# Selective-scan layer of a four-layer kernel: where the gate is multiplied, who splits B, which activation tables are loaded, how many variance buffers there are

## The chip, the cores and the metric

The kernel runs on one core of a Trainium2 chip. The metric is the device time of one launch in microseconds (us). One launch computes four layers one after the other; the change is in the first.

## What is computed

Four layers map x, of shape 8 x 64 x 64 x 64 (images, channels, rows, columns), to the output. Layer 0 is a selective scan over the 4096 places of each image, followed by a gated norm; layers 1 and 3 are attention layers, layer 2 adapts a small network by gradient steps. What matters here is layer 0's core (cut):

```python
xz = jnp.einsum('bhwc,dc->bhwd', x, in_proj_w) + in_proj_b      # x is layer-normed
xi, z = jnp.split(xz, 2, axis=-1)                               # 128 channels each
xc = jax.nn.silu(_dwconv3(jnp.transpose(xi, (0, 3, 1, 2)), conv_w, conv_b))
...                       # xs: four directions (rows, columns, and both reversed)
x_dbl = jnp.einsum('bkdl,kcd->bkcl', xs, xproj_w)
dts, Bs, Cs = jnp.split(x_dbl, [R, R + N], axis=2)              # R = 4, N = 16
dts = jax.nn.softplus(jnp.einsum('bkrl,kdr->bkdl', dts, dtproj_w) + dtproj_b)
# for each place t, channel c and state n:
h = h * jnp.exp(dt_t[..., None] * A) + dt_t[..., None] * B_t[:, :, None, :] * u_t[..., None]
y = jnp.einsum('bkcn,bkn->bkc', h, C_t)
...
y = _ln(y, outnorm_g, outnorm_b, LN_EPS) * jax.nn.silu(z)       # the gate
return jnp.einsum('bhwd,cd->bhwc', y, outproj_w) + outproj_b
```

## The kernel before, in words

**Units and steps.** `scan_layer` works on eight images. Each has four directions k (in the order 0, 2, 1, 3; the last image 1, 3, 0, 2), and each direction four chunks of 1024 places: 16 steps per image. A step handles the 16 states n one by one; each is a unit on tiles of 128 channels x 1024 places:

- `load` (L729): one row of B (`bt`) or C (`ct`) is read from DRAM and spread over 128 partitions, 512 KB; SyncE's queue issues it, five buffers for `ct`, two for `bt`.
- `decay` (L733): ScalarE computes a = exp(dt * A_n), three buffers.
- `spread` (L751): TensorE makes B_n on all partitions out of three bf16 parts of B (`bs`, 48 rows) into the PSUM tile z, two buffers. For the states in `BY_POOL` (0, 3, 6, 8) GpSimd multiplies `bt` by dt*u instead (`product`, L741) and ScalarE copies that to z (L748).
- `unit` (L778, L782, L787): VectorE multiplies z by dt*u (not for `BY_POOL`), then scans h = a*h + z; GpSimd multiplies h by `ct`.
- `sum_up` (L848): TensorE adds the result to the PSUM tile `yps`, two units later; `save_state` (L769) keeps the last column for the next chunk.

The order of work is written out by hand (`tc.manual_schedule()`): every engine gets its instructions in the order of the program. The main loop runs ahead for some operations (`spread` one unit, `decay` two, `product` three).

**Background.** Everything else hangs in a queue of small items (`Background`). In each unit at most one item gives TensorE its matmuls (`make`, called in `bg.before`), and one unit later its result is used (`use`, in `bg.after`); what was put off with `bg.later` goes out in the `bg.after` of the same unit for a `make`, one unit later for a `use`. In the units listed in `idle` (6, 7, 8) no item with a `make` is taken. Items share two PSUM banks (tag `mm`). They are, in the order of an image: eight loads of x into `xn` and its layer norm (`norm_x`), the projection into the padded image `pad`, the gates, the convolutions in groups of nine taps (L544) with Silu (L553), and, when the next image has begun (step 0, unit 4), the norm and output of the finished one (`after`, `norm_y`).

**The gate before.** `gate(j)` (L520 on): a matmul of win and the block of `xn` (L524), Silu on ScalarE (L529) into an SBUF tile z, which goes by DMA to the DRAM tile `zd`. Eight blocks per image, before the convolutions. In `after`, `load` brings a block of `zd` back (and a block of x, `xr`), GpSimd multiplies it by the normed y (L580), and `project_out` (L586, L587) adds x by the identity and multiplies by wout.

**The norm of y.** `inverse_root`: for each block a row of variances is put from PSUM into the SBUF tile `vrow` (L344, ScalarE) and sent to DRAM (L345, one unit later). That tile shares the tag `rstd`, with one buffer, with the row that is read back. Then the variances are read as 128 partitions, Sqrt (L355), reciprocal (L358), and back. `norm_y` multiplies y by the inverse root (L460, VectorE, out of PSUM) and applies gain and offset (L461).

**The next step's inputs.** `prepare` queues `project` as the first items of a step: B and C (`dps`, L619, for k < 2, which also serves k + 2), dt as Relu and Abs (L647, L648). In the units 6, 7, 8 the rest of softplus follows: exp (L653), ln(1 + .) (L656), the sum on GpSimd (L659); dt*u at unit 11 (L678). For k < 2 `pieces` splits B into three bf16 parts in the units 7 to 13: fetch (L687), first part (L691, ScalarE), remainder (L695, GpSimd), second part (L698, ScalarE), third (L701, GpSimd), store (L706), get (L713). In the first three steps of image 0 (`early`) all of this stands in the units 12 to 15.

**Tables.** [...] These loads are placed by the compiler: in the code before one at each ln, one at the exp after it, one at each Silu and Sqrt and one at the exp after these.

Of the kernel before, what the change touches and what calls it, by code (L numbers as in the profile page):

```python
# [10 lines left out]
F32 = mybir.dt.float32  # L11
# [7 lines left out]
NB = 8  # L19
# [222 lines left out]
def scan_layer(cm, x_in, w, xh):  # L242

    tc, nc = cm.tc, cm.nc
    with ExitStack() as ctx:
# [73 lines left out]
        eps = cm.tile([128, 1], "eps")  # L319
        nc.vector.memset(eps, 1e-5)  # L320
        pick = cm.pool.tile([3 * N, N], BF16, name="pick", tag="pick")
        rows = work.tile([3 * N, N], F32, name="rows", tag="vsm")
# [5 lines left out]
        nc.gpsimd.memset(pad, 0.0)  # L328
        bg = Background()

        def bank(name):
# [4 lines left out]
        def inverse_root(nb):  # L336

            var = dr.tile([L], F32, name="vard", tag="vard")[: nb * BK]
            rs = dr.tile([L], F32, name="rsd", tag="rsd")[: nb * BK]
            sm = {}  # L340

            def put(ps, n, at):
                t = work.tile([NBK, BK], F32, name="vrow", tag="rstd", bufs=1)
                nc.scalar.copy(t[:n], ps[:n])  # L344
                bg.later(lambda: nc.sync.dma_start(  # L345
                    var[at * BK : (at + n) * BK].rearrange("(o n) -> o n", o=n), t[:n]
                ))

            def fetch(_):

                sm["v"] = work.tile([128, TQ], F32, name="vsm", tag="vsm")[:, : nb * BK // 128]
                nc.sync.dma_start(sm["v"], var.rearrange("(p f) -> p f", p=128))

            def root(_):
                nc.scalar.activation(sm["v"], sm["v"], AF.Sqrt, bias=eps)  # L355

            def invert(_):
                nc.vector.reciprocal(sm["v"], sm["v"])  # L358
                bg.later(lambda: nc.sync.dma_start(rs.rearrange("(p f) -> p f", p=128), sm["v"]))

            def back(_):
                sm["r"] = work.tile([NBK, BK], F32, name="rstd", tag="rstd", bufs=1)[:nb]
                nc.sync.dma_start(sm["r"], rs.rearrange("(j f) -> j f", j=nb))

            chain = [none, (None, fetch), none, none, (None, root), (None, invert), none]
            chain += [(None, back), none, none, none]
            return put, chain, sm
# [57 lines left out]

        def norm_y(y, blocks, load, multiply, project_out):

# [7 lines left out]
            def variance(j):  # L435
                def make():
                    ps = bank("vps1")
                    nc.tensor.matmul(
                        ps[:1], lno_avg[:, NBK - 1 : NBK], sq.pop(j), start=True, stop=True
                    )  # L440
                    return ps

                def use(ps):
                    put(ps, 1, j - j0)
                    if j + 2 in blocks:
                        square(j + 2)

                return make, use

            def apply(j):  # L450
# [7 lines left out]
                def use(ps):  # L458
                    v = y[:, bass.ts(j, BK)]
                    nc.vector.tensor_tensor(v, v, ps, ALU.mult)  # L460
                    nc.scalar.activation(v, v, AF.Identity, bias=on_b, scale=on_g)  # L461
                    if j - 1 in blocks:
                        multiply(j - 1)

# [3 lines left out]
            for j in blocks:  # L468
                out.append(variance(j))
                if j in blocks[1:6:2] or nb == 2:  # L470
                    at = j if nb == 2 else j0 + (j - j0) // 2
                    out.append((None, lambda _, at=at: load(at)))
            out += chain
            out += [apply(j) for j in blocks[:2]]
            end = (None, lambda _: multiply(blocks[-1]))
            if nb == 2:
                out += [end, none]
            for j in blocks:
                if j + 2 in blocks:
                    out.append(apply(j + 2))  # L480
                    if j + 2 == blocks[-1]:
                        out.append(end)
                out += [project_out(j), none]
            return out
# [4 lines left out]
        def before(b):  # L489

            xn = io.tile([2 * C, NBK // 2, BK], F32, name="xn", tag="xn", bufs=1)

# [3 lines left out]
            u = io.tile([DI, L], F32, name="u", tag="u")  # L496
            zd = dr.tile([DI, L], F32, name="zd", tag="zd")
            rows = BK // S
# [6 lines left out]
            def project_in(j):  # L505
# [6 lines left out]
                def use(ps):  # L512
# [3 lines left out]
                    )  # L516

                return make, use

            def gate(j):  # L520
                def make():
                    ps = bank("zps")
                    half, x = block(j)
                    nc.tensor.matmul(ps, win[half, 1, :], x, start=True, stop=True)  # L524
                    return ps

                def use(ps):
                    z = work.tile([DI, BK], F32, name="z", tag="z", bufs=3)
                    nc.scalar.activation(z, ps, AF.Silu, bias=inb[:, 1:2])  # L529
                    bg.later(lambda: nc.sync.dma_start(zd[:, bass.ts(j, BK)], z))  # L530

                return make, use

            def convolve(j):
# [17 lines left out]
                def use(_):  # L552
                    nc.scalar.activation(u[:, bass.ts(j, BK)], held[0], AF.Silu, bias=convb)  # L553
                    if b:
                        bg.done[b] += 1
# [6 lines left out]
            for pairs in FIRST if b == 0 else (range(NBK // 2),):  # L562
                items.append(norm_x(b, xn, pairs, project_in))
            return u, zd, items, [gate(j) for j in range(NBK)], [convolve(j) for j in range(NBK)]

        def after(b, y, zd, blocks=range(NBK)):

# [3 lines left out]
            def load(j):  # L571
                xr = work.tile([C, BK], F32, name="xr", tag="xr", bufs=3)
                nc.sync.dma_start(xr, xf[:, bass.ts(j, BK)])
                z = work.tile([DI, BK], F32, name="z", tag="z", bufs=3)
                nc.sync.dma_start(z, zd[:, bass.ts(j, BK)])
                gated[j] = (xr, z)

            def multiply(j):
                z = gated[j][1]
                nc.gpsimd.tensor_tensor(z, z, y[:, bass.ts(j, BK)], ALU.mult)  # L580

            def project_out(j):
                def make():
                    po = bank("ops")
                    xr, z = gated[j]
                    nc.tensor.matmul(po[:C], cm.ident[:C, :C], xr, start=True, stop=False)  # L586
                    nc.tensor.matmul(po[:C], wout, z, start=False, stop=True)  # L587
                    return po
# [10 lines left out]

            return norm_y(y, blocks, load, multiply, project_out)  # L600

# [78 lines left out]

        def pieces(ctl, low):

# [31 lines left out]

            return ([fetch, first, subtract, second, third, store] if ctl["k"] < 2 else []) + [get]

# [152 lines left out]
        def prepare(b, s):  # L869
# [18 lines left out]
            )  # L888
            ctl["pieces"] = pieces(ctl, low)
            return ctl  # L890
# [5 lines left out]
        def start(b):  # L896
            u, zd, items, gates, convs = before(b)
            images[b] = {"u": u, "zd": zd}
            bg.add(items[0] + items[1])
            if b == 0:  # L900
                bg.add(convs[0] + convs[1])
                for s in range(1, NCH):
                    later[s] = sum(items[s + 1 : s + 2], []) + convs[2 * s] + convs[2 * s + 1]
                later[NCH] = gates
            else:
                bg.done[b] = 0
                bg.add([(None, lambda _: bg.groups.extend(deque(conv) for conv in convs))])
                bg.add(gates)


        with tc.manual_schedule():
            start(0)
            bg.drain()
# [13 lines left out]
            for b in range(NB):  # L927
                for s in range(4 * NCH):
# [29 lines left out]
                    for n in range(N):  # L958
# [30 lines left out]
                        if s == 0 and n == LAG + 2 and b > 0:  # L989
                            last = images.pop(b - 1)  # L990
                            bg.add(after(b - 1, last["row"], last["zd"]))
                            bg.add([(None, lambda _, b=b - 1: bg.flushed.add(b))])
                        if late and n == LAG + 2:
                            c = 4 * NCH - s
                            bg.add(after(b, images[b]["row"], images[b]["zd"], range(2 * c, 2 * c + 2)))
                        if s == (1 if b else NCH) and n == 0 and b + 1 < NB:
                            bg.add(later.pop(NCH, []))
                            start(b + 1)
# [8 lines left out]
            last = images[NB - 1]  # L1007
            bg.add(after(NB - 1, last["row"], last["zd"], range(2)))
            bg.drain()
# [1148 lines left out]
```

## Time and profile before

| | us |
|---|---|
| median of three runs | 12334.72 (12313.69 to 12336.37) |
| profiled execution | 12328.75, its span 12326.7 |
| scan layer in the span | 0 to 7053: before the first scan 94.4, eight images 920.8, 853.4, 856.3, 847.7, 859.6, 849.9, 871.6, 864.9, after the last scan 34.4 |
| other three layers | 5273.7 |
| busy in the span: PE, DVE, ACT, POOL | 11203.1, 10359.2, 7820.8, 7399.3 |
| middle of the scan layer (1500 to 6500 us): DMA | 64% busy, 207 to 215 GB/s |

In all views PE is TensorE (PEld its weight loads), DVE VectorE, ACT ScalarE, POOL GpSimd and SP the SyncE queue that issues all the DMAs. A group's row gives line, engine, operation, output and inputs with their shapes, the count, then busy time in us and mean in ns, then the idle time just before these instructions with what ended it. A window's row gives its bounds and length, the busy time of each engine with the number of instructions, the clock granted to TensorE, the DMA share and GB/s. A timeline row gives start, duration, engine, line and operation, with the idle time before it in brackets. Windows of images and steps begin at the first scan of each.

### The profile page before, as it was taken

The page shows a single profiled execution, that of the slowest core. Times are in us where ns is not written, and L with a number is a line of the kernel's source. Part 1 is how long each engine was busy: PE and PEld are TensorE (multiplying, and loading weights), DVE is VectorE, ACT ScalarE, POOL GpSimd, SP SyncE. Part 2 cuts the span into 40 slices and gives each one's busy share as a digit, 9 for nine tenths or more (in the row PEclk, how much of TensorE's full clock was granted, in tenths as well). Part 3 has the DMA queues.
Part 4 walks back from the last instruction along what each step waited for, and adds up shares of the span by engine and source line. Part 5 has one row for each costly group of instructions (what it writes and reads, how often), then busy time and mean ns, then how long its engine had stood idle before and what let it go on. Part 6 is the DMA issues. An engine that isn't in the chain of part 4 may idle for free. (4 is left out here: it accounts for less than half of the span.)

```text
span 12326.7 us, 120038 instructions
## 1 busy us (share of the span) xinstructions
PE 11203.1 (91%) x38827; PEld 4075.9 (33%) x38827; DVE 10359.2 (84%) x7334; ACT 7820.8 (63%) x10409; POOL 7399.3 (60%) x3510
## 2 busy tenths in 40 slices
PE   7899999999999999999998899999987779999999
PEld 2233332332332332333322233232335463333333
DVE  5999999999999999999999776868677686676767
ACT  4776776776766766767766554646547574555554
POOL 5999999999999999999999700000006480000000
PEclk8999999999999999999999899999998789999999
DMA  3666666666666666666666400000011100000000
GB/s 115 207 213 218 209 209 217 219 203 216 218 210 213 211 210 217 213 215 213 199 213 211 164 24 26 5 25 7 17 41 41 41 21 24 19 4 19 5 11 6
DMA packets 541331, 1562.16 MB, mean 127 GB/s; under 512 B 127360, under 2 KB 144400, under 8 KB 538128
## 3 DMA queue, kind: packets, MB, share of 16 engines
q1 hardware_dynamic: 540688, 1554.36, 38.5%
q8 instruction: 309, 5.06, 0.2%
q14 instruction: 334, 2.74, 0.1%
HBM read 1456.41 MB, written 88.87 MB: 125 GB/s over the span
## 5 line engine op out<-in xcount | busy, mean ns | idle before, releaser
L787 POOL TENSOR_TENSOR ct<-ct,h 128x1024 f32<-128x1024 f32 x2048 | 4794.6, 2364 | 248.2 <-DVE h L782 113.3
L782 DVE TENSOR_TENSOR_SCAN h<-a,state,z 128x1024 f32<-128x1024 f32 x1536 | 3573.1, 2342 | 118.2 <-ACT z L748 67.1
L1159 DVE TENSOR_TENSOR sum<-sum,ex 128x1024 f32<-128x1024 f32 x1920 | 2347.5, 1223 | 618.1 <-ACT ex L1152 484.4
L1152 ACT ACTIVATE ex<-sc 128x1024 f32<-128x1024 f32 x2048 | 1968.1, 1024 | 1359.6 <-PE sc L1147 1359.6
L848 PE MATMUL yps<-ct,ident 128*128 128x512 f32 x5632 | 2809.0, 630 | 2.5 <-POOL ct L787 2.4
L733 ACT ACTIVATE a<-dt,amat 128x1024 f32<-128x1024 f32 x2048 | 2345.4, 1147 | 725.9 <-DVE h L782 712.5
L778 DVE TENSOR_TENSOR z<-z,e 128x1024 f32<-128x1024 f32 x1536 | 1863.3, 1213 | 221.1 <-PE z L751 143.2
L1166 PE MATMUL av<-ex,v 128*64 128x512 f32 x8192 | 1950.0, 604 | 0.0
L1147 PE MATMUL sc<-q,k 16*128 16x512 f32 (+1 forms) x8192 | 1562.2, 623 | 4.2 <-ACT q L1140 3.1
L848 PEld LDWEIGHTS yps<-ct,ident 128*128 128x128 f32 x5632 | 1006.4, 194 | 1384.2 <-issue 1220.6
L751 PE MATMUL z<-bs,pick 48*128 48x512 bf16 x3072 | 948.0, 389 | 536.5 <-DVE h L782 485.5
L848 PE MATMUL yps<-ct,lno_cen 128*128 128x512 f32 x2560 | 1276.3, 630 | 0.0
L782 DVE TENSOR_TENSOR_SCAN h<-a,z 128x1024 f32<-128x1024 f32 x512 | 1162.7, 2282 | 81.4 <-ACT z L748 57.2
L741 POOL TENSOR_TENSOR bt<-bt,e 128x1024 f32<-128x1024 f32 x512 | 1210.1, 2364 | 5.3 <-DMA bt<-bc 5.3
L1473 POOL TENSOR_TENSOR gt<-gt,pad 128x1024 f32<-128x1024 f32 x16 | 34.9, 2179 | 1570.2 <-ACT gt L1472 1570.2
L1166 PEld LDWEIGHTS av<-ex,v 128*64 128x64 f32 x8192 | 512.2, 136 | 1332.8 <-issue 1278.9
L1147 PEld LDWEIGHTS sc<-q,k 16*128 16x128 f32 (+1 forms) x8192 | 528.4, 184 | 1016.2 <-issue 977.3
L748 ACT COPY z<-bt 128x1024 f32<-128x1024 f32 x512 | 519.8, 1015 | 537.5 <-POOL bt L741 334.8
L751 PEld LDWEIGHTS <-pick 48*128 48x128 bf16 x3072 | 177.6, 95 | 1754.9 <-DVE h L782 1003.0
L848 PEld LDWEIGHTS yps<-ct,lno_cen 128*128 128x128 f32 x2560 | 458.1, 193 | 618.3 <-issue 564.2
L544 PE MATMUL vps<-pad,convd 128*128 128x512 f32 x1152 | 550.9, 602 | 12.9 <-ACT e L648 12.9
L1846 DVE RECIPROCAL r<-e 128x512 f32<-128x512 f32 x128 | 420.7, 3323 | 0.0
(416 smaller groups left out, 10449.5 us busy)
## 6 DMA issues: line engine op xcount, KB each, us to landing
ct<-bc SPq DMA_DIRECT2D x2048, 512.0 KB
bt<-bc SPq DMA_DIRECT2D x512, 512.0 KB
x<-x SPq DMA_DIRECT2D x12, 2048.0 KB
bc<-e SPq DMA_DIRECT2D x128, 128.0 KB
zd<-z SPq DMA_DIRECT2D x64, 256.0 KB
z<-zd SPq DMA_DIRECT2D x64, 256.0 KB
x<-x SPq DMA_DIRECT2D x32, 512.0 KB
part<-x SPq DMA_DIRECT2D x128, 128.0 KB
```

The lines of the kernel that those rows point to most:

```text
L544: nc.tensor.matmul(held[0].rearrange("p (r c) -> p r c", c=S), convd[:, t, :], pad[:, j * rows + dy : (j + 1) * rows + dy, dx : dx + S], s ...
L733: ctl["exp", n] = nc.scalar.activation(ctl["a", n], ctl["dt"], AF.Exp, scale=amat[:, ctl["k"], n : n + 1])
L741: nc.gpsimd.tensor_tensor(bt, bt, ctl["dus"], ALU.mult)
L751: nc.tensor.matmul(z[:, bass.ts(i, BK)], pick[:, n : n + 1].to_broadcast([3 * N, DI]), ctl["bs"][:, bass.ts(i, BK)], start=True, stop=True,)
L778: first = nc.vector.tensor_tensor(z, z, ctl["dus"], ALU.mult)
L782: nc.vector.tensor_tensor_scan(h[:, flip], a[:, flip], z[:, flip], 0.0 if state is None else state[:, n : n + 1], ALU.mult, ALU.add,)
L787: freed[at] = nc.gpsimd.tensor_tensor(ct, ct, h, ALU.mult)
L848: nc.tensor.matmul(ctl["ps"][:, bass.ts(i, BK)], ctl["mat"], ct[:, bass.ts(i, BK)], start=False, stop=(n == N - 1 and not ctl["turns"]),)
L1147: nc.tensor.matmul(sc[:, e, :], k[r : r + d, bass.ts(j, 128)], qs[i][r : r + d, :], start=True, stop=True,)
L1152: nc.scalar.activation(ex, sc, AF.Exp)
L1159: nc.vector.tensor_tensor(sums[i], sums[i], ex, ALU.add)
L1166: nc.tensor.matmul(avs[i][r, :], v[:, j, r], ex[:, e, :], start=(j == 0), stop=(j == TQ - 1))
```

## The change

Five edits, all in `scan_layer`:

1. The gate is no longer computed ahead and kept in DRAM. `gate(j)` moves into `after`: the matmul goes to a PSUM bank, Silu is applied in place in PSUM (put off with `bg.later`, so after the decay of the same unit), and one unit later VectorE multiplies y by it out of PSUM. `zd` and both its DMAs are gone, and `xn` has two buffers, since it is needed until then.
2. For k < 2 (but not in the early steps) B's second and third parts are made by TensorE: identity times B minus the parts so far (`minus`, bf16), then copied by ScalarE to bf16. The pieces stand at the units 5, 7, 8, 9, 10 and 13, and unit 9 is idle for the background too.
3. `exp_and_ln` loads the set of tables with exp and ln; it is called at the start and after each Silu and Sqrt. In the changed program no other load stands before an exp or an ln.
4. `vrow` has a tag of its own with two buffers; `inverse_root`'s chain has one empty item fewer.
5. The order of the items in `norm_y` follows: loads of `xr` inside the first three variances, a gate between the norm of a block and its output.

```diff
+        minus = cm.pool.tile([128, 128], BF16, name="minus", tag="minus")
+        nc.vector.tensor_scalar(minus, cm.ident, -1.0, None, ALU.mult)
...
+        def exp_and_ln():
+
+            nc.scalar.add_instruction(mybir.InstLoadActFuncSet(
+                name=nc.get_next_instruction_name(), act_func_set_id=6, engine=mybir.EngineType.Activation,
+                ins=[], outs=[],
+            ))
...
             def put(ps, n, at):
-                t = work.tile([NBK, BK], F32, name="vrow", tag="rstd", bufs=1)
+                t = work.tile([NBK, BK], F32, name="vrow", tag="vrow", bufs=2)
...
                 nc.scalar.activation(sm["v"], sm["v"], AF.Sqrt, bias=eps)
+                exp_and_ln()
...
-            chain += [(None, back), none, none, none]
+            chain += [(None, back), none, none]
...
                     if j + 2 in blocks:
                         square(j + 2)
+                    if j - j0 < 3:
+                        load(j)
...
-                    if j - 1 in blocks:
-                        multiply(j - 1)
...
-            out += [apply(j) for j in blocks[:2]]
-            end = (None, lambda _: multiply(blocks[-1]))
-            if nb == 2:
-                out += [end, none]
+            out += [apply(j) for j in blocks[:2]] + [gate(j0)]
             for j in blocks:
                 if j + 2 in blocks:
                     out.append(apply(j + 2))
-                    if j + 2 == blocks[-1]:
-                        out.append(end)
-                out += [project_out(j), none]
+                out += [gate(j + 1) if j + 1 in blocks else none, project_out(j)]
...
-            xn = io.tile([2 * C, NBK // 2, BK], F32, name="xn", tag="xn", bufs=1)
+            xn = io.tile([2 * C, NBK // 2, BK], F32, name="xn", tag="xn")
...
-                def use(ps):
-                    z = work.tile([DI, BK], F32, name="z", tag="z", bufs=3)
-                    nc.scalar.activation(z, ps, AF.Silu, bias=inb[:, 1:2])
-                    bg.later(lambda: nc.sync.dma_start(zd[:, bass.ts(j, BK)], z))
...
                     nc.scalar.activation(u[:, bass.ts(j, BK)], held[0], AF.Silu, bias=convb)
+                    exp_and_ln()
...
-                z = work.tile([DI, BK], F32, name="z", tag="z", bufs=3)
-                nc.sync.dma_start(z, zd[:, bass.ts(j, BK)])
-                gated[j] = (xr, z)
-
-            def multiply(j):
-                z = gated[j][1]
-                nc.gpsimd.tensor_tensor(z, z, y[:, bass.ts(j, BK)], ALU.mult)
+                gated[j] = xr
+
+            def gate(j):
+                def make():
+                    ps = bank("zps")
+                    half, x = block(j)
+                    nc.tensor.matmul(ps, win[half, 1, :], x, start=True, stop=True)
+
+                    def silu():
+                        nc.scalar.activation(ps, ps, AF.Silu, bias=inb[:, 1:2])
+                        exp_and_ln()
+
+                    bg.later(silu)
+                    return ps
+
+                def use(ps):
+                    v = y[:, bass.ts(j, BK)]
+                    nc.vector.tensor_tensor(v, ps, v, ALU.mult)
...
+            def rest(i):
+                def do():
+                    ps = bank("brps")
+                    b, p = (low[n] for n in "bp")
+                    nc.tensor.matmul(ps[:, :256], cm.ident, b.rearrange("p a x -> p (a x)"), start=True, stop=False)
+                    for q in range(i):
+                        nc.tensor.matmul(
+                            ps[:, :256], minus, p[:, q].rearrange("p a x -> p (a x)"),
+                            start=False, stop=(q == i - 1),
+                        )
+                    nc.scalar.copy(p[:, i].rearrange("p a x -> p (a x)"), ps[:, :256])
+
+                return do
+
+            if ctl["k"] >= 2:
+                return [get]
+            if early:
+                return [fetch, first, subtract, second, third, store, get]
+            return [fetch, first, rest(1), rest(2), store, get]
...
-                    idle = () if early or late else (6, 7, 8)
+                    parts = nxt and not early and nxt["k"] < 2
+                    idle = () if early or late else (6, 7, 8, 9) if parts else (6, 7, 8)
...
-                            hooks = {14 - len(do) + i: [f] for i, f in enumerate(do)}
+                            hooks = dict(zip((5, 7, 8, 9, 10, 13) if parts else (13,), ([f] for f in do)))
```

More of the change, by code (lines that the diff above doesn't have):

```diff
@@ L424, in norm_x, with norm_y @@
             return out
-        def norm_y(y, blocks, load, multiply, project_out):
+        def norm_y(y, blocks, load, gate, project_out):
             put, chain, sm = inverse_root(len(blocks))
@@ L469, in norm_y @@
                 out.append(variance(j))
-                if j in blocks[1:6:2] or nb == 2:
-                    at = j if nb == 2 else j0 + (j - j0) // 2
-                    out.append((None, lambda _, at=at: load(at)))
             out += chain
-            out += [apply(j) for j in blocks[:2]]
-            end = (None, lambda _: multiply(blocks[-1]))
-            if nb == 2:
-                out += [end, none]
+            out += [apply(j) for j in blocks[:2]] + [gate(j0)]
             for j in blocks:
@@ L496, in before @@
             u = io.tile([DI, L], F32, name="u", tag="u")
-            zd = dr.tile([DI, L], F32, name="zd", tag="zd")
             rows = BK // S
@@ L516, in use @@
                     )
[L518 to L525, printed above, removed]
-                def use(ps):
-                    z = work.tile([DI, BK], F32, name="z", tag="z", bufs=3)
-                    nc.scalar.activation(z, ps, AF.Silu, bias=inb[:, 1:2])
-                    bg.later(lambda: nc.sync.dma_start(zd[:, bass.ts(j, BK)], z))
                 return make, use
@@ L563, in before, with after @@
                 items.append(norm_x(b, xn, pairs, project_in))
-            return u, zd, items, [gate(j) for j in range(NBK)], [convolve(j) for j in range(NBK)]
-        def after(b, y, zd, blocks=range(NBK)):
+            return u, block, items, [convolve(j) for j in range(NBK)]
+        def after(b, y, block, blocks=range(NBK)):
             xf = x_in[b].rearrange("c h w -> c (h w)")
@@ L573, in load @@
                 nc.sync.dma_start(xr, xf[:, bass.ts(j, BK)])
-                z = work.tile([DI, BK], F32, name="z", tag="z", bufs=3)
-                nc.sync.dma_start(z, zd[:, bass.ts(j, BK)])
-                gated[j] = (xr, z)
-            def multiply(j):
-                z = gated[j][1]
-                nc.gpsimd.tensor_tensor(z, z, y[:, bass.ts(j, BK)], ALU.mult)
+                gated[j] = xr
[12 more added lines that the diff above has]
+                    nc.vector.tensor_tensor(v, ps, v, ALU.mult)
+                return make, use
             def project_out(j):
@@ L584, in make @@
                     po = bank("ops")
-                    xr, z = gated[j]
-                    nc.tensor.matmul(po[:C], cm.ident[:C, :C], xr, start=True, stop=False)
-                    nc.tensor.matmul(po[:C], wout, z, start=False, stop=True)
+                    v = y[:, bass.ts(j, BK)]
+                    nc.tensor.matmul(po[:C], cm.ident[:C, :C], gated[j], start=True, stop=False)
+                    nc.tensor.matmul(po[:C], wout, v, start=False, stop=True)
                     return po
@@ L598, in project_out @@
                 return make, use
-            return norm_y(y, blocks, load, multiply, project_out)
+            return norm_y(y, blocks, load, gate, project_out)
         def ordered(t, k, c):
@@ L678, in step_input, with pieces @@
             nc.gpsimd.tensor_tensor(ctl["dus"], ctl["dt"], ctl["ut"]["u"], ALU.mult)
-        def pieces(ctl, low):
+        def pieces(ctl, low, early):
             by_place = "a n (j x) -> (n j) a x"
@@ L713, in get @@
                 nc.sync.dma_start(ctl["bs"], low["bsd"][ctl["k"] // 2])
-            return ([fetch, first, subtract, second, third, store] if ctl["k"] < 2 else []) + [get]
+            def rest(i):
[15 more added lines that the diff above has]
+            return [fetch, first, rest(1), rest(2), store, get]
         BY_POOL = (0, 3, 6, 8)
@@ L888, in prepare @@
             )
-            ctl["pieces"] = pieces(ctl, low)
+            ctl["pieces"] = pieces(ctl, low, b == 0 and s < NCH)
             return ctl
@@ L896, in start @@
         def start(b):
-            u, zd, items, gates, convs = before(b)
-            images[b] = {"u": u, "zd": zd}
+            u, block, items, convs = before(b)
+            images[b] = {"u": u, "x": block}
             bg.add(items[0] + items[1])
@@ L903, in start @@
                     later[s] = sum(items[s + 1 : s + 2], []) + convs[2 * s] + convs[2 * s + 1]
-                later[NCH] = gates
             else:
@@ L907, in start @@
                 bg.add([(None, lambda _: bg.groups.extend(deque(conv) for conv in convs))])
-                bg.add(gates)
         with tc.manual_schedule():
+            exp_and_ln()
             start(0)
@@ L990, in scan_layer @@
                             last = images.pop(b - 1)
-                            bg.add(after(b - 1, last["row"], last["zd"]))
+                            bg.add(after(b - 1, last["row"], last["x"]))
                             bg.add([(None, lambda _, b=b - 1: bg.flushed.add(b))])
@@ L994, in scan_layer @@
                             c = 4 * NCH - s
-                            bg.add(after(b, images[b]["row"], images[b]["zd"], range(2 * c, 2 * c + 2)))
+                            bg.add(after(b, images[b]["row"], images[b]["x"], range(2 * c, 2 * c + 2)))
                         if s == (1 if b else NCH) and n == 0 and b + 1 < NB:
-                            bg.add(later.pop(NCH, []))
                             start(b + 1)
@@ L1007, in scan_layer @@
             last = images[NB - 1]
-            bg.add(after(NB - 1, last["row"], last["zd"], range(2)))
+            bg.add(after(NB - 1, last["row"], last["x"], range(2)))
             bg.drain()
```

## The prediction

> **What bounds the kernel now.** First the page: busy shares and the 40 slices.
>
> ```profile
> PE 11203.1 (91%) x38827; PEld 4075.9 (33%) x38827; DVE 10359.2 (84%) x7334; ACT 7820.8 (63%) x10409; POOL 7399.3 (60%) x3510
> ...
> DVE  5999999999999999999999776868677686676767
> ...
> POOL 5999999999999999999999700000006480000000
> ```
>
> VectorE (DVE) and GpSimd (POOL) both stand at 9 from the second slice to the 22nd, and POOL is nearly idle after that: this stretch, up to 7053 us, is the scan layer, and only it is changed. The other 5274 us I leave alone. Next the windows of images 0 and 1 (each begins with the image's first scan), then those of steps 1, 3 and 11 of image 1's 16. The columns are the length, then PE, PEld, DVE, ACT and POOL busy.
>
> ```profile
> 94.40:1015.20 920.80, 820.22 (x1870) 286.79 (x1870) 816.39 (x458) 648.94 (x901) 822.41 (x367) 0.95 0.59 195
> 1015.20:1868.60 853.40, 793.14 (x1824) 270.30 (x1824) 818.22 (x464) 614.65 (x881) 835.79 (x377) 0.98 0.65 213
> ```
>
> ```profile
> 1066.87:1122.03 55.16, 48.20 (x113) 14.78 (x112) 50.92 (x29) 40.54 (x63) 53.66 (x25) 1.00 0.71 232
> ...
> 1175.28:1230.38 55.10, 52.07 (x119) 16.51 (x118) 53.20 (x33) 36.86 (x55) 55.10 (x28) 1.00 0.71 228
> ...
> 1602.40:1658.04 55.64, 52.48 (x122) 18.81 (x120) 51.08 (x30) 47.51 (x62) 51.68 (x23) 0.97 0.65 213
> ```
>
> An image takes 853 us; POOL works 835.8 of them and VectorE 818.2. POOL is the bound, by 17.6 us per image, and both lose some more to each other. In step 3 (55.10) POOL has no idle at all; in step 11 (55.64) both are idle for 4 us, while ACT is at 47.5. Last the groups of the scan layer, by engine, and a stretch of the timeline.
>
> ```profile
> L580 POOL TENSOR_TENSOR z<-z,y 128x512 f32<-128x512 f32 x64 | 81.5, 1273 | 23.3 <-ACT y L461 23.3
> L701 POOL TENSOR_TENSOR bp<-br,bp 128x256 bf16<-128x256 f32 x64 | 43.2, 675 | 2.1 <-ACT bp L698 2.1
> L695 POOL TENSOR_TENSOR br<-bw,bp 128x256 f32<-128x256 f32 x64 | 43.1, 674 | 0.0
> ```
>
> ```profile
> L460 DVE TENSOR_TENSOR y<-y,rps 128x512 f32<-128x512 f32 x64 | 42.2, 663 | 6.9 <-PE rps L455 6.9
> ```
>
> ```profile
> L733 ACT ACT_TABLE_LOAD x266 | 341.3, 1283 | 12.2 <-DVE h L782 7.8
> ...
> L656 ACT ACT_TABLE_LOAD x128 | 164.2, 1283 | 2.3
> ```
>
> ```profile
> 1085.63 0.57 ACT L344 COPY vrow<-vps 1x512 f32<-1x512 f32 x1
> ...
> 1089.07 0.24 SPq L345 DMA_DIRECT2D vard<-vrow  x1
> ...
> 1091.84 0.57 ACT L344 COPY vrow<-vps 1x512 f32<-1x512 f32 x1 [3.99 <-DMA vard<-vrow]
> ```
>
> The last three lines are step 1: the second variance row waits 3.99 us for the first one's DMA, because both use one buffer. Behind it on ACT stand a decay and the copy of z for unit 8, and VectorE then sits idle 3.60 us at that unit's scan. The same happens in step 6 (2.60 us); ACT's waits of this kind add to 108.5 us in 27 cases over the layer.
>
> [...] The trace has 1283; a separate drain does not show (the loads of L656 have 2.3 us of idle before them in 128 cases), so I use 1.28. [...] L460 reads PSUM, 663 ns for 512 columns, and the 1024-column product at L778, also from PSUM, takes 1213.
>
> **The change part by part.**
> *Gating.* POOL loses 64 products of 1273 ns (start to start 1227): 8 x 1.23 = 9.8 us per image, all in steps 2 to 4. VectorE gains 64 of L460's kind; one is followed by the next after 0.58: 8 x 0.58 = 4.6 per image. In the order of the changed program they stand in step 2 (unit 14), step 3 (2, 5, 11, 14) and step 4 (3, 9, 11). The 128 DMAs of 256 KB go from SP; its long waits are for free ct buffers, and the traffic is 2% of 1562 MB: I count zero. The gates' 128 loads stay but move from steps 9 to 11 into 2 to 4.
> *Remainders of B.* In 60 of 64 steps POOL loses 674 + 675 ns (start to start 2 x 627): 1.25 us. TensorE gains two fp32 products and three bf16 ones of 256 columns. None is in the trace. Half of L848's two passes of 0.43 and half of L751's 0.22 give 2 x 0.43 + 3 x 0.11 = 1.2 us per step. Below: nothing, since in units 9 to 15 TensorE waits for h (485.5 us at L751 in all). Above: all of it, 60 x 1.2 = 72 us. I take nothing. The remainders now make a chain ACT, PE, ACT, PE, ACT; what queues behind a waiting TensorE are the spreads of z two units ahead, and VectorE has no idle in those units. The fetch moves from unit 7 to 5, so SP may wait a DMA's time of 2 to 3 us with ct loads behind it; ct is loaded several units ahead, so also nothing, at most 32 x 1 us.
> *Tables.* Loads in the layer fall from 545 to 299 in the instruction order: 246 x 1.28 = 316 us of ACT. ACT is not the bound, so this counts only where ACT is late.
> *vrow.* Two buffers remove the two waits above; a third row in a row could still wait, but its DMA is then two units old. What is late next in step 1 is POOL's own work (53.66 of 55.16).
> *Banks.* A gate's PSUM bank, one of two, is now held until VectorE's product one unit later, but the next item to need it comes two units later: nothing.
>
> **The sum for an image of the middle** (image 1, 853.4). After the change POOL has 22 products of 128x1024 (2364 ns, start to start 2.315), 50.9 us per step (814.9 per image), VectorE 818.2 + 4.6 = 822.8. So the bound moves to VectorE and the floor falls only by 13.
> - Steps 0, 8, 10 (51.7, 50.3, 52.3; POOL full): POOL sheds 1.25, VectorE needs 50.0, 49.7, 51.0. I give 1.1 + 0 + 1.0 = 2.1.
> - Steps 1, 9, 11 (55.2, 54.9, 55.6), where vrow or the gates' loads made the idle: down to 52.3, about what the plain steps 5 and 12 to 15 take (52.6 mean, with convolutions). 2.9 + 2.6 + 3.3 = 8.8.
> - Steps 2 to 4 (53.3 + 55.1 + 54.5 = 162.8): VectorE has 156.8 + 4.6 = 161.5 and I add 1 for ACT's loads: gain 0.3. The 9.8 that POOL sheds here come to almost nothing.
> - Step 6: vrow's idle, 2.0. The six others: the two loads around the logarithm go from ACT, 0.2 each, 1.0.
> That is 14.2 for image 1; I take 13 for each of images 1 to 5: 65 us. Image 6, with two convolution groups per step beside the gates (871.6), 19. Image 0: its step 4 holds all eight gates (VectorE idle 7.7 us there), 5; three early steps with an exposed load, 4; vrow, 3; steps 8 to 11, 6; the rest and the start, 2: 20. Image 7: 4 (gains of 7, less 3 for the gates in its last steps). The tail after the last scan: two Silus with loads in the chain, +2. Sum 65 + 19 + 20 + 4 - 2 = 106.
>
> The profiled execution took 12328.75 (span 12326.7 and 2 around it), 6 under the median 12334.7; taken from the median: 12229.
>
> **Rivals.**
> A larger gain: the idle time left is mostly made by a late ACT, and VectorE comes near its own work. With 0.5 us idle per step an image takes 823 + 8 = 831: 22 x 7 + 25 = 179, so 12156. For: ACT sheds 2.5 us per step. Against: in steps 12 to 15 VectorE's idle is put to PE's z, with convolutions and POOL's products ahead of it, and both stay.
> Lost again: the remainders on TensorE (up to 72) hold up z, as PE already does in steps 9 to 15; gain 106 - 72 = 34, so 12301.
> Slower: VectorE, in order, waits for each gate's Silu, which has a table load before it and decays of ACT ahead; scans of the next units queue behind. Place: steps 2 to 4. From 106 / 64 = 1.7 us per gate on it eats the whole gain; at 3 us it costs 192, so 12421. Against: the multiply stands one unit after its Silu, some 3.5 us later, and steps 2 to 4 start with ACT at 34 to 37 us of 55.
> That loads stay is no rival: the instruction order has none before exp or ln.
>
> **Numbers.** Forecast 0.65; larger 0.14; lost again 0.13; slower 0.08. About 0.2% (25 us) is what can be told from no change. Faster: 0.65 + 0.14 + 0.08 of the third; same: its other 0.05; slower 0.08. The range goes from 12150 (larger gain) to 12302 (lost again), and leaves out the slower case and the tails.
>
> **What would show it.** Right: no table load at the logarithm; no wait of vrow for its DMA in step 1; POOL near 815 and VectorE near 823 per image, images 1 to 5 near 840; steps 9 and 11 down by 3, steps 2 to 4 as before. Wrong: VectorE idle before the gate's product, or z waiting behind the remainders in units 8 to 11.

## The result and the profile after

| | before | after |
|---|---|---|
| median (us) | 12328.95, six runs | 12268.2 (12262.15 to 12282.43), six runs |
| profiled execution, its span | 12328.75, 12326.7 | 12270.35, 12268.6 |
| scan layer: start, images 0 to 7 | 94.4; 920.8 853.4 856.3 847.7 859.5 849.9 871.6 864.9 | 92.2; 921.9 853.2 843.9 843.3 843.1 848.8 852.1 859.3 |

The ratio is 0.9952, with an interval of 0.9941 to 0.9963: faster by some 60 us, where 106 were forecast. The page of the changed kernel:

```profile
PE 11225.6 (91%) x39247; PEld 4130.5 (34%) x39247; DVE 10385.4 (85%) x7399; ACT 7517.0 (61%) x10224; POOL 7250.8 (59%) x3326
...
DVE  5999999999999999999999776868778676676767
...
POOL 4999999999999999999999600000006480000000
```

ACT sheds 304 us and POOL 149, and VectorE gains 26. Both bounding engines still stand at 9 through the whole layer. The windows of image 0, of image 1, of its steps 1, 3 and 11, and of step 3 of image 3; the last line, in a fence of its own, is step 3 of image 3 in the kernel before:

```profile
92.19:1014.10 921.91, 825.29 (x1891) 292.91 (x1891) 815.67 (x458) 559.84 (x829) 817.50 (x357) 0.94 0.57 190
1014.10:1867.29 853.19, 803.32 (x1862) 277.39 (x1862) 822.11 (x471) 573.26 (x855) 816.96 (x353) 0.97 0.63 208
1064.30:1115.89 51.59, 45.52 (x111) 15.47 (x111) 51.02 (x30) 35.22 (x56) 51.59 (x23) 0.99 0.66 225
1172.58:1230.13 57.55, 55.26 (x125) 17.39 (x124) 54.88 (x36) 44.31 (x63) 50.83 (x22) 1.00 0.58 199
1601.98:1654.39 52.41, 47.68 (x114) 17.43 (x114) 50.81 (x29) 34.34 (x49) 50.09 (x22) 1.00 0.62 208
2867.61:2929.07 61.46, 58.17 (x127) 18.16 (x126) 55.70 (x38) 45.01 (x63) 51.16 (x23) 0.94 0.54 184
```

```profile
2884.87:2939.49 54.62, 52.00 (x119) 16.51 (x118) 53.11 (x33) 36.76 (x55) 54.62 (x27) 1.00 0.71 231
```

Read them against the forecast: VectorE 822 and POOL 817 in image 1 (forecast 823 and 815), step 1 down from 55.2 to 51.6, step 11 from 55.6 to 52.4. But step 3 has risen, to 57.6 in image 1 and to 61.5 in image 3, where VectorE is busy for only 55.7 of it (53.1 of 54.6 before) and ACT for 45.0 instead of 36.8. The groups of loads and of the gate's product, then ScalarE's and SP's variance rows in step 1 of image 1:

```profile
L335 ACT ACT_TABLE_LOAD x150 | 192.4, 1283 | 3.3 <-PEq L2163 0.8
...
L571 ACT ACT_TABLE_LOAD x64 | 82.1, 1283 | 14.2 <-PE zps L568 13.1
...
L579 DVE TENSOR_TENSOR y<-zps,y 128x512 f32<-128x512 f32 x64 | 42.9, 670 | 9.3 <-ACT zps L571 8.8
```

```profile
1081.59 0.57 ACT L353 COPY vrow<-vps 1x512 f32<-1x512 f32 x1
...
1084.11 0.57 ACT L353 COPY vrow<-vps 1x512 f32<-1x512 f32 x1
...
1086.64 0.28 SPq L354 DMA_DIRECT2D vard<-vrow  x1
```

L335 is the explicit load; the layer has 299 loads, and no group of them stands at an exponential or a logarithm any more (L752, L654, L657; before, 266 at L733 and 128 at L656). The second variance row is copied 2.5 us after the first, before the first one's DMA is even issued: the wait of 3.99 us is gone. The gate's product takes 670 ns, and VectorE waited 9.3 us for all 64 together.

### The profile page after: what moved, and what is told of

It reads as the page before. It is cut to its first block, busy times and chain, and to the rows that moved or that the text cites. A ratio compares the mean times of both kernels' runs of the same rounds, so it can differ in the third digit from the quotient of the medians.

```text
span 12268.6 us, 120386 instructions
## 1 busy us (share of the span) xinstructions
PE 11225.6 (91%) x39247; PEld 4130.5 (34%) x39247; DVE 10385.4 (85%) x7399; ACT 7517.0 (61%) x10224; POOL 7250.8 (59%) x3326
## 5 line engine op out<-in xcount | busy, mean ns | idle before, releaser
L752 ACT ACTIVATE a<-dt,amat 128x1024 f32<-128x1024 f32 x2048 | 2346.8, 1147 | 1116.3 <-DVE h L801 1112.3
L867 PE MATMUL yps<-ct,ident 128*128 128x512 f32 x5632 | 2772.3, 622 | 0.0
```

Source lines behind the costliest of these rows:

```text
L752: ctl["exp", n] = nc.scalar.activation(ctl["a", n], ctl["dt"], AF.Exp, scale=amat[:, ctl["k"], n : n + 1])
L867: nc.tensor.matmul(ctl["ps"][:, bass.ts(i, BK)], ctl["mat"], ct[:, bass.ts(i, BK)], start=False, stop=(n == N - 1 and not ctl["turns"]),)
```

## The experiments

Ratios are to the kernel before, timed on the same chip, and a gain in us is the ratio's share of its time. Steps are means over images 1 to 5 of one profiled execution.

**Each part alone** (e1 to e4, each an edit of the kernel before).

e1, two buffers for the variance rows:

```diff
-                t = work.tile([NBK, BK], F32, name="vrow", tag="rstd", bufs=1)
+                t = work.tile([NBK, BK], F32, name="vrow", tag="vrow", bufs=2)
```

> The kernel before with one edit alone: two buffers for the variance rows. If ScalarE's wait for the rows' DMA is a cause of its own, steps 1 and 6 of images 1 to 6 shorten by some 3.5 and 2 us, together 30 to 40 us. If GpSimd is the bound whatever ScalarE does, only GpSimd's own idle time in these two steps comes back, 2.8 us per image, about 20 us.

Measured: 12309.16, ratio 0.9982 (0.9974 to 0.9991): 22 us. ScalarE waits for no row any more, and step 1 falls from 56.4 to 52.4, step 6 from 53.7 to 51.7, as a cause of its own would have it. But the others drift by up to 1.2 us, mostly upward, so that a whole image is only 0.7 shorter, and the total is nearer to the 20 of the other case.

e2, the explicit load of the set with exp and ln (edit 3):

```diff
                 nc.scalar.activation(sm["v"], sm["v"], AF.Sqrt, bias=eps)
+                exp_and_ln()
...
                    nc.scalar.activation(z, ps, AF.Silu, bias=inb[:, 1:2])
+                    exp_and_ln()
```

> The kernel before with one edit alone: the set with exp and ln, so that no load stands at the logarithm (245 loads fewer). If ScalarE is not the bound and its lateness matters little, 5 to 15 us. If a late ScalarE makes most of the idle time of the middle steps, 40 us or more.

Measured: 12315.93, ratio 0.9983 (0.9976 to 0.9990): 21 us, between the two cases. The profile has 150 loads at the explicit one (1283 ns each) and none at an exponential or a logarithm of the layer. The start and image 0 hold 6.9 of the gain and step 11 (55.0 to 52.8) 11; step 13 loses nearly 8 again.

e3, B's remainders by TensorE and ScalarE (edit 2):

```diff
-            return ([fetch, first, subtract, second, third, store] if ctl["k"] < 2 else []) + [get]
...
+            return [fetch, first, rest(1), rest(2), store, get]
```

> The kernel before with one edit alone: B's second and third parts by TensorE and ScalarE. If GpSimd is the bound, the 1.25 us that it sheds in each of 60 steps comes back, up to 75 us; with VectorE only 0 to 1.2 us behind it in those steps, 30 to 50. If the remainders hold up z on TensorE instead, no gain.

Measured: 12332.12, ratio 0.9998 (0.9989 to 1.0007): nothing. Steps 0, 1, 9 and 11 get shorter by 1.6, 3.7, 2.5 and 2.1, but step 12 rises from 51.4 to 57.7, step 4 by 2.1 and step 8 by 1.9. In step 1 it takes what e1 took: with one buffer still, ScalarE's waits for the rows' DMA fall from 108.5 us (27 cases) to 49.0 (17), in step 1 of images 1 to 5 from 52 to 8.

e4, the gate alone (edit 1 and the order of edit 5, with the chain as before):

```diff
-            return u, zd, items, [gate(j) for j in range(NBK)], [convolve(j) for j in range(NBK)]
+            return u, block, items, [convolve(j) for j in range(NBK)]
...
+                    v = y[:, bass.ts(j, BK)]
+                    nc.vector.tensor_tensor(v, ps, v, ALU.mult)
```

> The kernel before with one edit alone: the gate as in the changed kernel, multiplied by VectorE out of PSUM (two buffers for xn). If the stall in step 3 of the changed kernel (z late on TensorE, which waits for a PSUM bank and then runs at half its rate) belongs to the gate, steps 9 to 11 gain some 4 us per image and step 3 loses 5: no gain, within 15 us of before. If the gate is good by itself, as predicted, 30 to 40 us faster.

Measured: 12367.64, ratio 1.0028 (1.0016 to 1.0041): slower by 35. Steps 2 to 4 take 170.5 instead of 162.6, step 8 53.2 instead of 50.4, image 7 883.1 instead of 864.9.

The four add to -22 - 21 - 2 + 35 = -10, and the whole change gave -61. The four leave out the shorter chain (the second half of edit 4), which was not run by itself, so this gap alone doesn't prove that the parts depend on one another; e3 and e1 in step 1, and e11 below, do. Two runs take one part out of the changed kernel.

e5, all but the gate and the shorter chain (the gates, `zd` and GpSimd's multiply as before):

```diff
-            out += [apply(j) for j in blocks[:2]] + [gate(j0)]
+            out += [apply(j) for j in blocks[:2]]
+            end = (None, lambda _: multiply(blocks[-1]))
```

> The changed kernel with the gate as before (DRAM, GpSimd) and the longer chain of the norm; the three other edits stay. If the gate's part brings about nothing by itself, this is as fast as the changed kernel, within 15 us. If the gate's part carries the gain, it is 30 us or more slower; if it costs, faster than the changed kernel.

Measured: 12287.75, ratio 0.9958 (0.9941 to 0.9975). Inside the changed kernel the gate and the shorter chain together neither cost nor give anything that can be told (7 us by the two ratios, 20 by the medians). Step 3 is 55.6, but step 12 is 57.5, as in e3: the gates are still queued ahead of the convolutions, the background has one unit fewer, and in both traces one gate of each image slips into step 12 (before, steps 9 to 11 hold three, three and two; here and in e3 one, two and four). With the gates moved (after) step 12 takes 51.7.

e11, all but the remainders:

```diff
-            return [fetch, first, rest(1), rest(2), store, get]
+            return ([fetch, first, subtract, second, third, store] if ctl["k"] < 2 else []) + [get]
```

> The changed kernel with B's remainders back on GpSimd. If the parts added up, the remainders are worth 2 us and the time stays at 12270. Theory of interplay (the gate's costs in steps 2 to 4 and 14 are paid for only with the remainders off GpSimd, and the remainders help only with the gates out of steps 9 to 11): the time goes back to the gate alone less the gains of the tables and of the buffers, 12368 - 22 - 21 = 12325 (ratio 0.999), steps 0, 9 and 11 take 1 to 2 us more than in the changed kernel.

Measured: 12346.27, ratio 1.0013 (1.0006 to 1.0020). The remainders, worth 2 us alone, are worth 78 here (12346.27 against 12268.2; by the two ratios 75). The loss lies in steps 2 (57.6 against 54.1), 4 (+2.5), 6 (+2.2), 10 (+1.9), 0 (+1.6) and 7 (+1.5), and step 3 stays at 59.8. It is larger than the interplay that I had priced (12325), and of the steps named beforehand only step 0 got longer: 9 and 11 did not.

**Step 3** (edits of the changed kernel). My first theory was a PSUM bank: the output's matmul L587 stood 2.21 us behind the gate. The timeline of after, image 3, step 3, from unit 2 on:

```profile
2875.21 4.58 DVE L801 TENSOR_TENSOR_SCAN h<-a,state,z 128x1024 f32<-128x1024 f32 x2
...
2876.33 1.28 ACT L571 ACT_TABLE_LOAD   x1
2877.61 0.60 PE L770 MATMUL z<-bs,pick 48*128 48x512 bf16 x2 [0.99 <-DVE h L801]
2877.63 0.66 ACT L571 ACTIVATE zps<-zps,inb 128x512 f32<-128x512 f32 x1
...
2878.31 1.28 ACT L335 ACT_TABLE_LOAD   x1
2879.60 0.69 ACT L648 ACTIVATE dt<-tps,dtb 128x512 f32<-128x512 f32 x1
...
2880.43 1.96 PE L587 MATMUL ops<-xr,ident 64*64 64x512 f32 x2 [2.21 <-DVE y L579]
2880.76 1.07 ACT L836 COPY y<-yps 128x512 f32<-128x512 f32 x2
...
2884.22 3.29 PE L858 MATMUL yps<-u,skipd 128*128 128x512 f32 x4
...
2887.44 0.60 PE L770 MATMUL z<-bs,pick 48*128 48x512 bf16 x2
...
2888.18 1.23 DVE L797 TENSOR_TENSOR z<-z,e 128x1024 f32<-128x1024 f32 x1 [4.29 <-PE z L770]
```

The same place in the kernel before, image 3:

```profile
2892.47 4.59 DVE L782 TENSOR_TENSOR_SCAN h<-a,state,z 128x1024 f32<-128x1024 f32 x2
...
2893.48 0.68 ACT L647 ACTIVATE dt<-tps,dtb 128x512 f32<-128x512 f32 x1
...
2894.64 1.07 ACT L817 COPY y<-yps 128x512 f32<-128x512 f32 x2
...
2895.76 1.98 PE L839 MATMUL yps<-u,skipd 128*128 128x512 f32 x4 [0.28 <-ACT y L817]
...
2897.67 0.60 PE L751 MATMUL z<-bs,pick 48*128 48x512 bf16 x2
```

Count from the start of the two scans (first line of each). L836/L817 are the copies that empty `yps`, the one PSUM tile of the running sum; the next sum starts behind them (L858/L839), and the z of unit 5 stands behind that on TensorE. The copies end 3.2 us after the scan's start before, and 6.6 after; z begins at 5.2 before, and at 12.2 after. Ahead of the copies on ScalarE there are now a load, the Silu and a load: 1.28 + 0.66 + 1.28 = 3.2 us. But here the sum does not wait for the copies: they end at 2881.83, and L858 begins at 2884.22, straight behind the output's matmuls. TensorE's stop is L587, which the profile puts down to the gate's product (L579); over the layer it waited there for 20.0 us, at 15 of the 64 gates. And from L587 on two passes of TensorE take 1.96 us instead of the 1.07 of the same matmul in a step without a pause (image 1).

e6 puts the gate's Silu behind the dt that is queued with it:

```diff
-                    bg.later(silu)
+                    bg.behind.append(silu)
```

> The changed kernel with one difference: in a unit in which a gate's Silu and the use of the item before both go out, the use comes first and the Silu with its two table loads after it. Bank theory: in step 3 the Relu and Abs of dt no longer stand behind 3.2 us of Silu and loads, their PSUM bank is free earlier, the output's first matmul does not wait for the gate's product, TensorE keeps its rate, and step 3 falls from 60.5 to about 55.5: 30 to 40 us faster than the changed kernel. If step 3 is long because VectorE has 55.5 us of work and waits for a Silu, or because of the loads themselves, no change, or slower, since the Silu now comes later.

Measured: 12301.64, ratio 0.9974 (0.9963 to 0.9985), and step 3 at 60.0. That is some 30 us slower than the changed kernel, where 30 to 40 faster were expected. The output's matmul no longer waits for the product, but TensorE stands idle for 1.48 us at the z before it, and most of the following passes are as slow as in after (0.86 to 0.95 us each, 0.43 at full rate). So this wait isn't the only one that keeps step 3 long.

e7 brings the empty item of the chain back (edit 4's second half), and e8 does both:

```diff
-            chain += [(None, back), none, none]
+            chain += [(None, back), none, none, none]
```

> The changed kernel with the empty item back in the norm's chain. In the early steps of image 0 the product by the inverse root then comes half a unit later, and VectorE should wait 1 us less in step 0 and 2.5 us less in step 1: about 3 us in image 0's window, too little for the time of the whole. If the three early steps have another cause, image 0 stays at 922.

> Both together, Silu last and the empty item back. If they are independent, 33 to 43 us faster than the changed kernel, near 12230.

Measured: e7 12315.37 in a single run; e8 12286.96, ratio 0.9959 (0.9945 to 0.9973). Step 3 stays at 60.7 and 60.1, with every item one unit later. In e7 image 0 is 5.3 shorter, and steps 13 and 14 and image 7 are longer: 1.9, 1.4 and 13.4. The timeline of e7, image 3, step 3:

```profile
2872.48 4.58 DVE L801 TENSOR_TENSOR_SCAN h<-a,state,z 128x1024 f32<-128x1024 f32 x2
...
2874.65 1.06 ACT L836 COPY y<-yps 128x512 f32<-128x512 f32 x2
...
2877.70 1.92 PE L568 MATMUL zps<-xn,win 64*128 64x512 f32 x2 [2.21 <-DVE y L472]
...
2879.55 3.78 PE L858 MATMUL yps<-u,skipd 128*128 128x512 f32 x4
```

The copies are back in time, 3.2 us after the scans' start, in this image and in images 2 to 5 of e7, and yet the step takes 60.0 to 61.7: TensorE now stops at the gate's own matmul, which waits 2.21 us for VectorE's product by the inverse root (L472), and is slow behind it (1.92 us for two passes, 3.78 for the four of the sum). Late copies are thus not needed for a long step 3.

e7 also differs from e5 by the gate alone: step 3 takes 60.7 with it and 55.6 without, step 12 51.7 and 57.5, and the scan layer of the one profile is 10 us longer than that of the other. From the changed kernel it differs by the empty item alone: its scan layer is 32 us longer, most of the rest of the 47 lies in the other layers. With the Silu last the sign is the other: e8, expected near 12230, is slower than the changed kernel too, but 15 faster than e6.

My second theory was half rate: that the pauses of TensorE slow the passes behind them. In after the matmuls of two passes take 1.96 us behind the pauses and 1.07 in a step without one; by the clock's record the slow stretch lasts 6.83 us at a clock of 0.50, and the pauses ahead of it are 0.99 and 2.21 us, with one matmul of z between. e9 fills the pause of e6:

```diff
-                    nc.tensor.matmul(ps, win[half, 1, :], x, start=True, stop=True)
+                    for _ in range(3 if j == 1 and len(blocks) > 2 else 1):
+                        nc.tensor.matmul(ps, win[half, 1, :], x, start=True, stop=True)
```

> The variant with the Silu behind the dt, and in it the gate's matmul of the second block (step 3, unit 2) issued three times instead of once, each time from zero, so that the result is the same and TensorE has 1.7 us more to do where it stood idle for 1.48 us. Theory (the pause sends TensorE to half rate, and that makes z late): the eight passes after it take 0.43 instead of 0.86 to 0.95, the clock granted in step 3 rises from 0.94 to about 1.00, VectorE's wait for z at unit 5 shrinks from 2.45 us to under 1, and step 3 of images 2 to 6 goes from 60.4 to about 57.5; total 6 x 3 = 18 under the variant's 12302, so about 12284 (ratio 0.996). Rival (the order of ScalarE and VectorE alone sets the step): the step stays at 60 or more and the total at 12302 to 12310.

Measured: 12304.12, ratio 0.9979 (0.9972 to 0.9986), step 3 at 61.4 (one image of the five at 67.4; images 2, 3 and 5 at 60.7 to 60.8, as in e6). The timeline of e9, image 3, step 3:

```profile
2876.05 2.84 PE L573 MATMUL zps<-xn,win 64*128 64x512 f32 x6
...
2879.19 1.07 PE L592 MATMUL ops<-xr,ident 64*64 64x512 f32 x2
2880.19 1.07 PE L593 MATMUL ops<-y,wout 128*64 128x512 f32 x2
...
2882.24 1.07 ACT L841 COPY y<-yps 128x512 f32<-128x512 f32 x2
...
2883.37 3.39 PE L863 MATMUL yps<-u,skipd 128*128 128x512 f32 x4 [2.10 <-ACT y L841]
...
2886.69 0.60 PE L775 MATMUL z<-bs,pick 48*128 48x512 bf16 x2
...
2887.43 1.23 DVE L802 TENSOR_TENSOR z<-z,e 128x1024 f32<-128x1024 f32 x1 [2.26 <-PE z L775]
```

The output's matmuls now run at full rate (1.07), and nothing is won: the start of the sum waits 2.10 us for the copies, and only then falls to half rate (3.39 for four passes, 1.98 in the kernel before). z comes 10.4 us after the scan's start, as late as in e6. In e9 half rate follows this pause of 2.10 us; what makes the pause in this kernel is ScalarE. What late copies go with can be read in step 13, where no gate stands: over images 1 to 5 of all kernels the step takes 52.4 to 53.2 us where they end 1.9 to 2.8 us after the start of unit 3's scan, 54.8 where it is 3.7, and 56.1 to 56.4 where it is 4.8 to 5.1. In after no image is late there, in e6 two are, in e9 all five (step 13: 53.2, 54.4, 56.3).

e10 puts products of a zero weight into the empty last units of steps:

```diff
+            for i in range(8):
+                nc.tensor.matmul(
+                    pending[0][0]["ps"][:, bass.ts(i % 2, BK)], zero,
+                    ctl["bs"][:, bass.ts(i % 2, BK)], start=False, stop=False,
+                )
```

> The changed kernel, with eight products of a zero weight added to the running sum in the last unit of a step where the background gives TensorE nothing (84 of 128 steps): 1.7 us of work without effect on the sum, where TensorE stands idle for 2.8 us. Theory that half rate at the starts of steps costs time: the loss of granted clock over the scan layer (length times one minus the clock) falls from 165 us to about 110, and the time falls by 15 to 45, to 12223 to 12253 (ratio 0.992 to 0.994). Rival (half rate at a step's start lies beside VectorE and GpSimd, which are the bound there): the clock rises and the time stays within 10 us of 12268. It would rise above 12280 if the added passes hold up the z behind them.

Measured: 12267.83, ratio 0.9948 (0.9929 to 0.9967): no change. The loss of clock (from the clocks of the steps' windows) fell only from 165 to 152 us, and not to 110, so that this run doesn't say what a higher clock would be worth.

**Image 0.** e12 brings the empty item back in image 0's own norm only:

```diff
-            out += chain
+            out += chain + [none] * (b == 0)
```

> The changed kernel with the empty item of the chain back for the first image's own norm alone. Theory (the 3.8 us that step 1 of image 0 lost, 78.9 to 82.8, come from the shorter chain: the inverse roots are asked for one unit too early and VectorE, in order, waits 2.5 us for them): step 1 of image 0 goes to about 79.0, the other steps of image 0 move by less than 1 us, images 1 to 7 stay as they are; total 12264 (ratio 0.995). Rival (step 1 is late through the loads of x and the convolutions of the first image): step 1 stays above 82.

Measured: 12266.54, ratio 0.9948 (0.9929 to 0.9967). The difference to after can't be told from the times, but in the profile it stands where it was expected. The window of image 0's step 1 in e12, and in after:

```profile
164.58:243.30 78.72, 64.82 (x146) 23.30 (x146) 52.26 (x30) 42.56 (x64) 52.48 (x25) 0.91 0.44 143
```

```profile
165.98:248.79 82.81, 67.31 (x146) 23.85 (x146) 52.37 (x30) 42.50 (x64) 52.54 (x25) 0.89 0.43 136
```

The same instructions, 4.1 us apart. Steps 0 to 2 of e12 are 5.6 shorter than those of after, and images 2 to 6 are as in after to 0.2 us. No version is faster than after by more than the intervals allow.

## Why the prediction was right, and where its sum was off

The direction, the engines' loads and most places of the gain were right, and the size was off by 48 of 106. Its own sum (gains, in us) beside the two profiles:

| part | forecast | measured |
|---|---|---|
| images 1 to 5 | 65 | 34.5 |
| image 6 | 19 | 19.5 |
| image 0 with the start | 20 | 1.1 |
| image 7 | 4 | 5.6 |
| after the last scan, other layers | -2 | -2.6 |
| sum | 106 | 58.1 |

And one image of the middle (mean of images 1 to 5):

| steps | forecast | measured |
|---|---|---|
| 0, 8, 10 | 2.1 | 2.3 |
| 1, 9, 11 | 8.8 | 7.4 |
| 2 to 4 | 0.3 | -5.4 |
| 6 | 2.0 | 1.6 |
| the six others | 1.0 | 1.0 |
| sum | 14.2 (13 taken) | 6.9 |

**Right.** The waits of vrow (steps 1 and 6, e1 by itself), the loads in step 11 (e2), the tail. Remainders on TensorE at nothing: in units 8 to 11 of the eight steps that make them (15, 0 to 2, 7 to 10) VectorE waits for no z in images 1 to 5; six of these steps got shorter, 2 and 15 longer by 1.1 and 0.8. The gate's product at the price of L460 (670 ns against 663), and VectorE's own wait for the Silu: 9.3 us in all, 0.15 per gate, where the slower rival needed 1.7.

**Partly luck.** Image 6 met its 19 although its step 3 lost 6.5 us, which the forecast did not have; its steps 10 and 11 gave 14.1. And image 1, on which the sum was worked out, gained 0.2 in place of 14.2: its steps 2 and 3 lost 5.8, its steps 7, 9 and 14 another 5.4.

**The step that failed** is "Steps 2 to 4 ... I add 1 for ACT's loads: gain 0.3". VectorE's own work was right, 161.0 us in these three steps where 161.5 were forecast. Its idle time was to fall to 1 and came to 6.8 (5.8 before): it left step 4 (3.2 to 0.8) and came back in step 3 (1.8 to 5.0), which went from 55.0 to 60.5. The sum took the three steps together, but with four gates VectorE's work in step 3 alone is 55.7, more than the step had taken. And it asked who waits for a gate's product on VectorE, not what stands behind the gate on the other engines. On ScalarE that is the rest of dt and the copies that empty `yps`, behind 3.2 us; on TensorE it is the output's matmul, for which the sum had no wait. TensorE stops there for 2.21 us and drops to half rate (1.96 us for two passes instead of 1.07), z for unit 5 comes late, and VectorE idles for 4.29 us. It was a wait of the kind that the slower rival described, on another engine and at few of the gates.

That the gate makes step 3 long is shown: with it the step takes 58.4 to 61.4 (after, e4, e6 to e12), without it 55.0 to 55.7 (before, e1, e2, e3, e5). Which of the waits is decisive is not: in after TensorE stops for a product of VectorE, in e9 for the copies, in e7 for another product with the copies in time, and with each the step is as long. In image 1 of after the first gate of step 3 falls at unit 4, behind the copies: the step takes 57.6 there at a clock of 1.00, and 1.7 of its 2.4 over before are VectorE's own (54.9 against 53.2 busy).

**Image 0.** The term "three early steps with an exposed load, 4" was wrong: with the empty item back (e12), steps 0 to 2 gain only 0.8 in all. The shorter chain, which the sum had at nothing, cost 5.6 us there, 4.1 of it in step 1. Step 4 gave its 5.6 (forecast 5). Steps 8 to 11 gave 0.4 instead of 6, and step 12 lost 3.2; no run settles why.

**What the sum could not have.** It priced each part by itself. Remainders alone give 2 us and in company 78; the gate alone costs 35, and in company, with the shorter chain, nothing that can be told. Each edit moves the units at which the other items fall. The traces show it whole for step 12, where the remainders push one gate out of steps 9 to 11. For most of the 78 us of e11 the cause stays open, and so does the worth of the shorter chain, which the sum had at nothing: 32 us of the scan layer by the one run of e7, and the other sign with the Silu last.

## What to carry to other kernels

When work moves to another place in a fixed order, list for each of its instructions what stands behind it on its own engine, and follow that to the next engine: in e9 a Silu between two table loads (3.2 us) delayed a copy, the copy a PSUM tile, the tile a matmul (2.10 us), and the matmul everything else on TensorE. A profile shows one late wait at a time; e6, e7 and e9 each removed one and found the next. Forecast the idle time that is left step by step: taken over three steps it looked like nothing, and one step held it. And where items take turns in shared slots, measure the edits in company: sums of single runs can have the wrong sign.

## What the runs showed of the hardware

Two pauses of TensorE of 0.99 and 2.21 us, with one matmul of z between, were followed by half rate: in after, image 3, matmuls of two passes took 1.96 us instead of 1.07, over 6.83 us. In e6 slow passes (0.86 to 0.95 us instead of 0.43) set in about a microsecond after a single pause of 1.48 us. In image 1, where the pause doesn't arise, the granted clock of step 3 is 1.00 instead of 0.94 for nearly the same matmuls (125 instead of 127).

A pause of 1.48 us is not enough by itself: of 40 pauses of 1.3 to 1.6 us in the scan layer of after, 3 were followed within 3 us by passes at half rate. In after half rate went with TensorE's busy share of fixed stretches. In the clock's record of that run, 240 entries, the rate is 1.00 or 0.50, and each change stands at a multiple of 3.41 us from the first entry. Cut the eight images into these stretches and take those at full rate: of 48 with TensorE busy for less than half, 44 were followed by half rate; of 82 with 50 to 70%, 13; of 1781 with more, 5. In step 3 of image 3 the stretch before (2876.64 to 2880.05) holds 0.60 us of matmuls, 18%, and the two behind it have a clock of 0.50. And each of the 63 stretches after which the full rate came back was busy throughout. The counts are of this one trace.
